# Sorting positions by tile before the first layer, instead of scattering rows to slots after the last

## The chip, the core and the metric

The kernel runs on one core of a Trainium2 chip. The metric is the device time of one execution in microseconds (us). The profile gives for one profiled execution the span from the first to the last instruction on that core, and what each engine and each transfer did in it. PE is TensorE, DVE is VectorE, ACT is ScalarE, POOL is GpSimd, and SP is SyncE, which only issues transfers here.

## The reference

x has 2 batches of 1024 positions of 256 features; the context has 77 rows of 192 features in each batch. Four blocks follow one another, each added to its input:

```python
x = x + xattn0(layernorm(x), ctx)      # 16 heads of 16
x = x + ffn0(layernorm(x))             # one expert, 256 -> 1024 -> 256, then its own layernorm
x = x + xattn1(layernorm(x), ctx)      # one head of 256, layernorms inside
# ffn1: a matrix per position, chosen by the position alone
scores = pe @ sign(tile_sigs).T        # (1024, 8)
idx = argmax(scores, axis=-1)          # one of 8 tiles for each position, the same in both batches
y_all = einsum('bsd,tod->bsto', layernorm(x), W) + b
x = x + y_all[b, s, idx[s]]
```

The last block has 8 matrices of 256 x 256. A position needs only the product with the matrix of its tile. Everything is float32. Which tile a position has depends on `tile_sigs`, an input, so it is worked out on the chip, but it does not depend on x.

## The kernel before, in words

The 2048 positions are worked on in 8 chunks of 256 (`NC`), two blocks of 128 each (`NI`); chunks 0 to 3 are batch 0, chunks 4 to 7 batch 1. Each chunk passes through `attention0`, `ffn0`, `attention1`, and then through `to_slots` (chunks 0 to 6) or `by_every_tile` (chunk 7). These are Python generators with a place in a queue (`begin`); `run` takes the generator with the lowest place, emits its next instructions, and puts it back at the place that it yields. Chunk c has places near 2c, so neighbouring chunks overlap. The instructions' order on each engine is then set by the framework's scheduler from this order of emission; at run time each engine follows its own order strictly, and so do SP's and POOL's transfers.

Names for reading the trace: `ps_q` (L580) is the query product of attention 0, `sc` its scores, `mx`, `pr`, `sm` its softmax, `pT` the transposed weights, `ps_o` and `ps_y` its output; `ps_h` and `ps_eo` (L676, L688) are the two products of ffn0; `xT_b`, `ps_s`, `ps_y1` belong to attention 1. `moments` makes mean and reciprocal deviation `rs` of a layernorm, on POOL (L196, L197) except for the last two chunks, where a chain of small VectorE operations does it (`inverse_root`). A suffix a, f, g, b or h on `rs`, `n` and `xT` says which layernorm it is: before attention 0, before and inside ffn0, before attention 1, before the last block.

x is loaded by plain transfers, chunk by chunk (L83). The first context (keys `kbd`, values `vbd`) is prepared beside chunk 0; the values of batch 1 take a path through HBM (`v_rows` to `ext`) and five multiplications on POOL (L321). The second context (`second_context`) and the choice of tiles (`choices`) come in the time of chunks 1 to 3.

The last block sorts rows by tile. `choices` computes for every position the row of a slot, so that each slot block of 128 rows holds one tile only. `zeros` writes zeros to all slots in HBM. `to_slots` scatters each block's normalized rows, its x plus bias, and its row number to the slots by an indirect transfer from POOL. `block` loads a slot block and the matrix of its tile (SP reads the matrix's row number from SBUF into a register, L777), transposes it on PE (`ps_yT`, L803), copies it on ACT (L805), multiplies (`ps_t`, L809), adds (L814) and scatters 128 rows to the output (L173). There are 15 such blocks for batch 0 and 13 for batch 1. The last chunk isn't sorted: `by_every_tile` multiplies it by all 8 matrices (`ps_z`, L834) and picks by a mask (L840); its weights `every` are one 2 MB load.

## Time and profile before

| what | value |
|---|---|
| times of three runs | 337.59, 339.75, 340.19 us; median 339.75 |
| the profiled execution: time / span | 340.51 us / 338.4 us |
| mean granted TensorE clock | 0.967 of full speed |
| busy: PE, DVE, ACT, POOL | 301.8, 211.0, 141.4, 130.6 us |
| PE products of the last block: ps_t, ps_yT, ps_z busy in the trace | 16.9 + 6.9 + 8.2, 11.6, 15.0 us |
| indirect transfers on POOL: out, slots, bias | 28 x 0.980, 14 x 1.019, 8 x 1.115 us |
| moved by DMA | 39.69 MB, mean 117 GB/s |

A busy time says how long an engine had something in work, not that it was the limit. An idle engine matters only where the chain of work that ends last runs through it. The three busy times of `ps_t` belong to three buffers for its weights (wt, wt_vbd, wt_w); matmuls overlap, so their busy times add up to more than the time that they take in a row. Each float32 product is two instructions in the trace: 128x128 by 128x256 in a full pipeline takes 0.43 us.

### The profile page before, as it was taken

How to read it: one execution, taken by the hardware profiler on the slowest of the kernel's cores; microseconds unless marked ns; L12 is line 12 of the kernel's file. 1: busy time of each engine (PE TensorE's matmuls, PEld its weight loads, DVE VectorE, ACT ScalarE, POOL GpSimd, SP SyncE). 2: the span in 40 equal slices, each digit the busy share in tenths (PEclk: the TensorE clock that was granted, in tenths of full speed). 3: DMA queues.
4: the chain of work that ended last, by engine and by line, in shares of the span. 5: the costliest groups of instructions: out<-in, count | busy, mean ns of one | idle time of the engine just before them, and what ended most of it. 6: DMA issues, size and time to landing. Idle time of an engine off the chain costs nothing.

```text
span 338.4 us, 6080 instructions
## 1 busy us (share of the span) xinstructions
PE 301.8 (89%) x2144; PEld 247.6 (73%) x2144; DVE 211.0 (62%) x624; ACT 141.4 (42%) x309; POOL 130.6 (39%) x183
## 2 busy tenths in 40 slices
PE   2979789999799899999999999999799996578995
PEld 2656568888488678877887888888688885455884
DVE  2278884695459657929757784894346659326343
ACT  2246566535234457365464744645324421212110
POOL 3104560424003458346435512432652716415422
PEclk9999999999899999999999999999999999559999
DMA  7597299999401302701000100250845687164510
GB/s 198 197 334 184 104 241 139 213 158 76 39 0 44 115 13 93 255 32 45 20 2 0 64 0 2 69 182 1 252 133 183 204 253 254 64 186 128 167 34 16
DMA packets 23209, 39.69 MB, mean 117 GB/s; under 512 B 2669, under 2 KB 9354, under 8 KB 23180
## 3 DMA queue, kind: packets, MB, share of 16 engines
q1 hardware_dynamic: 19788, 32.22, 38.3%
q0 software_dynamic: 2848, 6.57, 5.9%
q10 hardware_dynamic: 544, 0.52, 0.5%
q8 instruction: 17, 0.28, 0.4%
q14 instruction: 12, 0.10, 0.1%
HBM read 25.52 MB, written 15.62 MB: 122 GB/s over the span
## 4 chain that ended last, share of the span: by engine, by line
PE 63%; DVE 18%; issue 7%; DMA 4%; POOL 3%; ACT 2%; SPq 1%; POOLq 0%; ACTq 0%
PE ps_eo L688 15%; PE ps_h L676 11%; PE ps_t L809 5%; PE ps_pT L634 4%; PE ps_z L834 4%; PE ps_y L656 4%; DVE mx L608 3%; PE ps_q L580 3%; DVE pr L610 3%; PE ps_o L643 2%; PE ps_s L721 2%; PE sc L599 2%; PE ps_y L746 2%; DMA wt<-in_wrow 2%; DMA wk<-in_wk 2%
## 5 line engine op out<-in xcount | busy, mean ns | idle before, releaser
L676 PE MATMUL ps_h<-xT_f,w 128*128 128x256 f32 x256 | 63.3, 390 | 3.0 <-issue 2.1
L688 PE MATMUL ps_eo<-w,hT 128*128 128x256 f32 x256 | 58.4, 381 | 1.9 <-ACT hT L681 1.9
L676 PEld LDWEIGHTS ps_h<-xT_f,w 128*128 128x128 f32 x256 | 47.0, 192 | 11.6 <-issue 4.5
L688 PEld LDWEIGHTS ps_eo<-w,hT 128*128 128x128 f32 x256 | 47.5, 190 | 8.3 <-ACT hT L681 2.3
L173 POOL DMA_INDIRECT out<-res,blk x28 | 27.4, 980 | 38.1 <-DVE res L814 14.5
L681 ACT ACTIVATE hT<-ps_h,cols 128x256 f32<-128x256 f32 x64 | 27.1, 466 | 30.7 <-PE ps_h L676 30.6
L614 ACT ACTIVATE pr<-pr 128x616 f32<-128x616 f32 x32 | 22.9, 717 | 37.5 <-DVE pr L610 37.5
L608 DVE TENSOR_REDUCE mx<-sc 128x8 f32<-128x616 f32 x32 | 25.2, 788 | 5.3 <-PE sc L599 5.3
L635 ACT COPY pT<-ps_pT 128x512 f32<-128x512 f32 x48 | 25.4, 595 | 6.2 <-PE ps_pT L634 6.2
L750 DVE SCALAR_TENSOR_TENSOR x<-ps_y,sm,x 128x256 f32<-128x256 f32 x16 | 7.1, 479 | 29.7 <-PE ps_y L746 29.7
L617 DVE TENSOR_REDUCE sm<-pr 128x8 f32<-128x616 f32 x32 | 24.6, 781 | 1.4 <-ACT pr L614 1.0
L610 DVE TENSOR_TENSOR pr<-sc,mx 128x616 f32<-128x616 f32 x32 | 25.2, 787 | 0.2
L805 ACT COPY yT<-ps_yT 128x256 f32<-128x256 f32 x28 | 10.4, 371 | 35.2 <-PE ps_yT L803 35.2
L634 PE MATMUL ps_pT<-ident,pr 128*128 128x128 f32 x160 | 21.0, 274 | 3.7 <-ACT pr L614 2.0
L566 POOL TENSOR_TENSOR x<-x,rows 128x512 f32<-128x512 f32 x16 | 21.0, 1321 | 8.3 <-ACT n_a L227 5.4
L634 PEld LDWEIGHTS ps_pT<-ident,pr 128*128 128x128 f32 x160 | 18.1, 141 | 5.9 <-ACT pr L614 2.5
L656 PE MATMUL ps_y<-wo,oT 128*128 128x256 f32 x64 | 17.4, 394 | 4.5 <-DVE oT L650 4.5
L765 POOL TENSOR_TENSOR both<-x,bias 128x256 f32<-128x256 f32 x14 | 9.9, 725 | 24.6 <-DVE x L750 24.5
L643 PE MATMUL ps_o<-pT,vbd 128*32 128x128 f32 x512 | 19.0, 283 | 0.1
L643 PEld LDWEIGHTS ps_o<-pT,vbd 128*32 128x32 f32 x512 | 14.4, 112 | 5.7 <-issue 4.5
L809 PE MATMUL ps_t<-wt,yT 128*128 128x256 f32 x60 | 16.9, 403 | 1.8 <-ACT yT L805 1.3
L173 POOL DMA_INDIRECT slots<-both,to x14 | 14.3, 1019 | 9.2 <-DVE both L232 2.7
(196 smaller groups left out, 545.8 us busy)
## 6 DMA issues: line engine op xcount, KB each, us to landing
blk<-slots SPq DMA_DIRECT2D x28, 256.5 KB
slots<-zero SPq DMA_DIRECT2D x1, 3847.5 KB
wt<-in_wrow SPq DMA_DIRECT2D x15, 256.0 KB
slots<-zero SPq DMA_DIRECT2D x1, 3334.5 KB
w<-in_w SPq DMA_DIRECT2D x2, 1024.0 KB
every<-in_wrow SPq DMA_DIRECT2D x1, 2048.0 KB
wt_w<-in_wrow SPq DMA_DIRECT2D x8, 256.0 KB
x<-in_x SPq DMA_DIRECT2D x7, 256.0 KB
```

The costliest lines, as they stand in the source:

```text
L173: i = nc.gpsimd.indirect_dma_start(out=to, out_offset=bass.IndirectOffsetOnAxis(ap=index, axis=0), in_=rows_in, in_offset=None, bounds_che ...
L608: nc.vector.tensor_reduce(mx, scv, AX.X, ALU.max)
L610: nc.vector.tensor_tensor(p8.rearrange("p (j h l) -> p j h l", j=4, l=L), scv, mx.unsqueeze(3).to_broadcast([P, 4, 2, L]), ALU.subtract,)
L617: nc.vector.tensor_reduce(sm[:, g * 8 : g * 8 + 8], pr[:, g, :G8].rearrange("p (h l) -> p h l", l=L), AX.X, ALU.add,)
L634: nc.tensor.transpose(ps[:, j * P : (j + 1) * P], srcs[4 * n + j], ident)
L635: nc.scalar.copy(pT[:, n].rearrange("p j t -> p (j t)"), ps)
L643: nc.tensor.matmul(ps[32 * m : 32 * m + 32, g * P : (g + 1) * P], vbd[:, e, n, g, 32 * m : 32 * m + 32], pTs[:, g * NK + n, :], start=n == ...
L656: nc.tensor.matmul(ps[:, :D], oT[:, g, :], wo[:, g, :], start=g == 0, stop=g == KC - 1)
L676: nc.tensor.matmul(ps[:, j, :], w1[:, k, (f + j) * P : (f + j + 1) * P], tT[:, k, :], start=k == 0, stop=k == KC - 1,)
L681: nc.scalar.activation(hT[-1][:, j, :], ps[:, j, :], AF.Relu, bias=col(C_B1 + f + j))
L688: nc.tensor.matmul(ps[:, :D], hT[f // 2][:, f % 2, i * P : (i + 1) * P], w2[:, f, :], start=f == 0, stop=f == F // P - 1,)
L809: nc.tensor.matmul(ps[:, :D], yT[:, k * P : (k + 1) * P], w[:, k * D : (k + 1) * D], start=k == 0, stop=k == KC - 1,)
```

## The change

The choice of tiles comes first (place -4), with the second context beside it. From the one-hot choice, `choices` computes the sorted order of the 1024 positions: where each position goes (`at`), and by a product of two comparisons which position stands at each place (`who`). x is then gathered in sorted order by indirect transfers on POOL (`rows_of_x`, two per chunk), in place of the plain loads; chunks alternate between the batches (`e = c % B`). All four layers work on sorted positions.

In sorted order a block of 128 positions has its tiles next to one another, so a batch has at most 8 + 7 = 15 pairs of a block and a tile (`NJ`). `pairs` computes the block (`block_i`), the matrix (`tile_i`) and the output rows (`to`) of each pair; rows that belong to another pair get a number beyond the output and are not written. `to_pairs` normalizes a chunk, transposes it on PE and keeps the result (`nT_of`) and x plus bias (`y_of`) in SBUF for all blocks. `pair` then copies the block's nT and y from there to its own buffers, by transfers whose source is given by a register, loads the matrix, multiplies, adds, and scatters to the output. The slots, their zeros, the blocks' transposes, and the dense products with `every` are gone. The 30 pairs are issued on SP as their chunk is done, and their products stand at the places `LATE`, near the end.

```diff
-    xs = [load("x_0", [P, NI, D], x_in[0], nc.scalar)]
-    xs += [load(f"x_{c}", [P, NI, D], x_in[c]) for c in range(3, NC)]
+    xs = [work.tile([P, NI, D], F32, tag="x", name=f"x_{c}", bufs=6) for c in range(NC)]
...
+    def rows_of_x(c):
+        e, s0 = c % B, c // B * NI
+        for i in range(NI):
+            gather(
+                xs[c][:, i, :], a["x"].rearrange("b s d -> (b s) d"),
+                chosen["who"][:, e, s0 + i : s0 + i + 1],
+            )
...
-    def to_slots(c, x):
+    def to_pairs(c, x):
         b = 2 * c
-        e, s0 = divmod(c * NI, NS)
+        e, s0 = c % B, c // B * NI
         m = moments(x, NI, f"h{c}", vector=c >= NC - 2)
+        written(
+            nc.gpsimd.tensor_tensor(
+                y_of[e][:, s0 : s0 + NI, :], x, bias[:, s0 : s0 + NI, :], ALU.add
+            ), e,
+        )
         yield b + 8.3
...
+        n = normed(x, NI, D, f"h{c}", m, act=True)
         yield b + 8.6
...
+        ps = bank(f"ps_xT_h{c}").rearrange("p (i k t) -> p i k t", i=NI, k=KC)
+        for i in range(NI):
+            for k in range(KC):
+                nc.tensor.transpose(ps[:, i, k, :], n[:, i, k * P : (k + 1) * P], ident)
+        written(
+            nc.scalar.copy(
+                nT_of[e][:, s0 : s0 + NI, :], ps.rearrange("p i k t -> p i (k t)")
+            ), e,
+        )
+
+    def pair(e, p, place):
+        n = f"{e}_{p}"
+        w = work.tile([P, KC * D], F32, tag="wt", name=f"wt_{n}", bufs=WT)
+        nT = work.tile([P, KC * P], F32, tag="nTp", name=f"nTp_{n}", bufs=NP_)
+        y = work.tile([P, D], F32, tag="yp", name=f"yp_{n}", bufs=NP_)
         first = nc.sync.value_load(
-            chosen["row"][0:1, e, j : j + 1], min_val=0, max_val=(NT - 1) * P
+            chosen["row"][0:1, p : p + 1], min_val=0, max_val=(NT - 1) * P
         )
         nc.sync.dma_start(w, a["wrow"][bass.ds(first, P), :])
...
+        lo, hi = max(0, p - NT + 1), min(p, NS - 1)
+        at = nc.sync.value_load(chosen["block"][0:1, p : p + 1], min_val=lo, max_val=hi)
+        readers[e].append(nc.sync.dma_start(y, y_of[e][:, bass.ds(at, 1), :]).ins)
+        readers[e].append(nc.sync.dma_start(nT, nT_of[e][:, bass.ds(at, 1), :]).ins)
+        yield place
         ps = bank(f"ps_t_{n}")
         for k in range(KC):
             nc.tensor.matmul(
-                ps[:, :D], yT[:, k * P : (k + 1) * P], w[:, k * D : (k + 1) * D],
+                ps[:, :D], nT[:, k * P : (k + 1) * P], w[:, k * D : (k + 1) * D],
                 start=k == 0, stop=k == KC - 1,
             )
...
+        r = work.tile([P, D], F32, tag="res", name=f"res_{n}", bufs=4)
+        nc.vector.tensor_tensor(r, ps[:, :D], y, ALU.add)
+        scatter(out, chosen["to"][:, e, p : p + 1], r, "out", B * S - 1)
+
+    LATE = (19.0, 19.2, 19.4, 19.6, 19.8, 20.0, 21.0, 22.8)
 
     for c in range(NC):
         begin(-1.4 if c == 1 else 2 * c - 2, attention0(c, xs[c]))
         begin(2 * c + 2.7, ffn0(c, xs[c]))
         begin(2 * c + 6.1, attention1(c, xs[c]))
-        begin(2 * c + 8.1, (to_slots if c < NC - 1 else by_every_tile)(c, xs[c]))
...
+        begin(2 * c + 8.1, to_pairs(c, xs[c]))
+    begin(-4, paced(-4, 0.4, choices()))
+    begin(-3.9, paced(-3.9, 0.4, first_context()))
+    begin(-3.7, paced(-3.7, 0.4, second_context()))
+    begin(-2.45, once(rows_of_x, 0))
+    begin(-2.4, once(rows_of_x, 1))
+    begin(-3.2, paced(-3.2, 0.2, values()))
+    begin(-1.8, paced(-1.8, 0.1, values_by_head()))
+    for c in range(2, NC):
+        begin((-0.6, 0, 1, 2, 8.7, 10.7)[c - 2], once(rows_of_x, c))
...
+    for c in range(NC):
+        e, j = c % B, c // B
+        ps = range(NI * j, NI * j + NI) if j < NC // B - 1 else range(NI * j, NJ)
+        for n, p in enumerate(ps):
+            begin(2 * c + 8.7 + 0.02 * n, pair(e, p, LATE[c] + 0.1 * n))
```

`WT` is 8 and `NP_` is 5. The computations inside `choices` and `pairs` are small operations on tables of 8 to 128 columns: some 30 on VectorE in `choices`, the comparisons `hot` among them, and some 18 in `pairs`.

## The prediction

> **What bounds the kernel now.** I read the cores view first (one core, span 338.4 us, granted clock 0.967), then the page's busy slices, then the table of windows with its borders at TensorE's milestones: the start of each chunk's query product ps_q, the end of the last attention-0 block (240.84), the end of chunk 7's second FFN product ps_eo (277.44), the end.
>
> ```profile
> core 0: us, PE busy (x) PEld busy (x) DVE busy (x) ACT busy (x) POOL busy (x), PEclk, DMA share, GB/s
> 0.00:29.07 29.07, 19.86 (x127) 14.22 (x127) 12.96 (x37) 10.54 (x18) 5.11 (x23) 1.00 0.84 244
> 45.16:73.85 28.69, 27.92 (x231) 23.53 (x230) 20.71 (x44) 15.07 (x31) 7.65 (x10) 1.00 1.04 185
> 73.85:111.42 37.57, 35.44 (x268) 28.64 (x267) 25.22 (x77) 15.07 (x31) 7.75 (x10) 0.95 0.49 53
> 171.28:199.43 28.15, 27.77 (x229) 23.33 (x228) 19.75 (x54) 15.90 (x35) 11.93 (x17) 1.00 0.05 20
> 199.43:240.84 41.41, 41.03 (x322) 34.47 (x320) 26.73 (x75) 20.21 (x47) 15.78 (x24) 1.00 0.22 64
> 240.84:277.44 36.60, 34.20 (x180) 29.95 (x180) 20.02 (x75) 13.33 (x33) 17.14 (x20) 1.00 0.67 211
> 277.44:338.40 60.96, 46.10 (x205) 36.86 (x203) 30.69 (x115) 9.92 (x26) 23.12 (x24) 0.85 0.40 125
> ```
>
> From 45 to 277 us PE is full: 27.77 of 28.15 us in a steady chunk, so work taken off PE there is time. The ends are chains: until the second ps_q PE computes 19.9 of 29.1 us, much of it cold, and after 277.44 it has 46.1 of 61.0 us at clock 0.85. DMA is full only early. The timeline shows the prices I need:
>
> ```profile
> 10.79 3.78 PE L580 MATMUL ps_q<-xT_a,wq 128*128 128x256 f32 x8 [0.68 <-ACT xT_a L257]
> 29.07 1.99 PE L580 MATMUL ps_q<-xT_a,wq 128*128 128x256 f32 x8
> 37.31 2.96 POOL L321 TENSOR_TENSOR vbd<-ext,cols 128x256 f32<-128x256 f32 x5 [2.48 <-DMA ext<-v_rows]
> 114.14 1.31 POOL L557 DMA_INDIRECT bias<-in_b,tid  x1 [0.18 <-issue]
> 115.75 0.95 POOL L557 DMA_INDIRECT bias<-in_b,tid  x1 [0.30 <-issue]
> 116.73 0.73 POOL L197 TENSOR_TENSOR rs_a<-rs_a,mhalf 128x2 f32<-128x2 f32 x1
> 290.32 0.47 PE L254 MATMUL ps_xT_b<-ident,n_b 128*128 128x128 f32 x1 [4.24 <-ACT n_b L227]
> 292.96 1.99 PE L721 MATMUL ps_s<-wqkg,xT_b 128*128 128x77 f32 x8
> ```
>
> A gather occupies POOL for about a microsecond and the next instruction starts only after it: rs_a stood behind two of them. After a 4.24 us gap PE runs at half pace (ps_s 1.99 us, elsewhere 1.05). The chain that ended last gives landings, and shows that it ended in the dense products ps_z:
>
> ```profile
> 281.00 5.15 DMA wt<-in_wrow
> 304.79 2.15 DMA out<-res,blk
> 310.32 2.83 DMA blk<-slots
> 331.20 3.47 PE ps_z L834 x16
> ```
>
> and the groups of the lines view the mean of one gather of 128 rows:
>
> ```profile
> L557 POOL DMA_INDIRECT bias<-in_b,tid x8 | 8.9, 1115 | 2.7 <-issue 1.5 <-DVE tid L478 1.2
> ```
>
> **What the Trainium skill says.** "TensorE: Matmul & The Clock Gate", section "Part 1: The HAM clock gate", says that PE falls to half clock after an idle window of about 3.4 us and rises again after as long a busy one; the 4.24 us gap and the doubled ps_s agree. Its opening table calls the queues of VectorE, ScalarE and GpSimd strict FIFO; rs_a behind the gathers agrees. "DMA: Bandwidth & Descriptors", section "Anatomy of one DMA", fits a software DMA by 2.0 us plus bytes over 436 GB/s: an estimate of 2.3 us for 128 KB. The nearest row, 2.83 us for a 256 KB block, is of that order.
>
> **The change part by part.** Instruction orders are those of the built kernel.
>
> *Head, until the second ps_q: 29.07 becomes about 57.0, +27.9 us.* x no longer arrives by a plain load (BN_STATS at 4.5); its row numbers must be computed first. Step by step: peT lands near 4 us; 16 choice products at cold pace, twice the 0.12 us each that they take warm, to 7.8; transposes of ctx to 8.5; VectorE copies cxT, does the statistics of ctx, then five choice operations of 0.2 us, to 10.9. PE then has, in its order, the count, ps_k (2.4 us cold, as before) and ps_v (2.7 before) ahead of ps_ahead: 17.2. Sixteen small VectorE operations, eight comparisons of 0.25 us, the who products and two more operations: the row numbers stand at about 22.4. POOL then does, in order, four gathers for x_0 and x_1 (1.115 busy + 0.30 issue = 1.41 each: 28.1), the five vbd products (2.96: 31.1; their ext rows need v_rows written and read back, each near 4.7 us as ext took, so by 27), five gathers for x_2, x_3 and half of x_4 (38.1), the first half of rs_a0, one more gather, and the power 0.72: 40.5. The statistics of x_0 wait since about 31, so the gathers queued ahead, not the data, set this. From the scale to the second ps_q: shift and normalization 1.4, transposes and copy 0.9, the cold ps_q 3.8 (the row at 10.79), qT behind two normalizations on ACT, scores to 8.2, then 8.2 for max, subtraction, exponential, sum, reciprocal, pT and ps_o: 16.5 us, so 57.0. The cover is none: nothing before x can run but the contexts, which are done by then. Ends: if row numbers stand at 18, +23; if POOL loses 2 us to ext, +30.
>
> *Middle, second to eighth ps_q: 170.4 becomes 158.6, -11.8 us.* The second context and the choices leave (PE 2.8 us in the stage from 45.16, 6.7 in that from 73.85, with some 2.5 us of waits on their VectorE rows): 28.7 to 26.3 and 37.6 to 28.6. Per chunk the transposes of n_h come in (0.43 us); ScalarE's 1.7 us for n_h and its copy lie in its idle half, and VectorE loses 0.86 us. POOL exchanges the slot scatters for the gathers of x_5 to x_7. Stages: 15.5, 26.3, 28.6, 30.0, 29.6, 28.6. Ends -9 (the gathers delay more scales) and -14. The 7.2 MB of zeros and `every` leave DMA, worth nothing where PE bounds.
>
> *Eighth ps_q to the end of ps_eo of chunk 7: 78.0 becomes 70.2, -7.8.* Nine blocks leave (9 x (0.865 product + 0.22 transpose) = 9.8), two pairs (1.7) and three transpositions (1.3) come in: -6.8; the 1.9 us that ps_eo waited for hT behind the slot scatters falls to 0.9. Ends -5 and -9: without blocks to fill it, PE now waits on the chain of g6 and b6, by my schedule under 1 us.
>
> *From there to the end: 61.0 becomes 57.0, -4.0.* Off PE go the rest of the blocks and 32 dense products (13.8 us); 28 pairs of 0.865 us stay. But these pairs are fed late: nTp and yp have five buffers, wt eight, and SP, in order, stops at the sixth nTp until the first pair's product is done, so 22 pairs load here, three transfers each at 0.5 us of SP (five wt_vbd issues took 2.78). Counted from the end of ps_eo: VectorE's statistics of b7 wait for res of pair 1_4, to 10; the two root chains, the normalizations and copies to 18; ps_s1_7 cold 2; the nine pairs of batch 0 stand in PE ahead of ps_y1_7, the first half cold, the last waiting for its copy: 30.3; y1 and the h7 chain, cold again, to 38.6; then nine copies (2.83 us to the first) and nine pairs. There the scatters bind: 9 x 1.28 us on POOL, 2.15 to land, about 0.8 to close: 57.0. The copies inside SBUF are in no row: from 2.3 us (the skill's estimate) to 5.15 (a wt load in a crowd); four round trips lie in series, so -0.6 to +10.9. I take 2.83.
>
> **Sum.** +27.9 - 11.8 - 7.8 - 4.0 = +4.3 us on the profiled execution's 340.51 us: 344.8; on the median 339.75 it is 344.05. I take 344.5.
>
> **The rivals.**
> *The copies land ahead of need (faster).* If a copy takes little over 1.5 us, no in-order engine waits for one in the last stage and PE keeps its clock: ps_s1_7 -1.0, batch 0's pairs -2.4, the h7 chain -0.5, the first copy -0.5, the last pairs -0.9, VectorE's wait before b7 -3.0: -8.3, so 336.2. For it: out landed in 2.15 with its POOL time inside. Against: 2.83 and 5.15. It decides below 1.5 us.
> *The head is cheaper (no change).* If PE warms during the choice products and the VectorE operations overlap, row numbers stand at 18 and the sum is near zero: 339.7. For it: the products are close together; against: PE was cold until 15.7 us before.
> *The copies are slow.* At 5.15 us: 355.4. For it: 22 pairs x 0.52 MB plus 3.9 MB of scatters, 15 MB in 60 us, is the 253 GB/s of the busiest slices; against: the waits are spread.
>
> **How the numbers follow.** Forecast 0.40, slow copies 0.12, cheaper head 0.20, early copies 0.28. Slower by over 1% (about what a measurement of this kernel can tell from no change) 0.52, within 0.20, faster 0.28. The forecast's own range is 341 to 350. Low copies with a somewhat cheaper head reach 334; the slow copies 356.
>
> **What would show it.** Right: the second ps_q starts near 57, POOL full of DMA_INDIRECT from 22 to 40 with rs_a behind them, steady chunks of 28.6, and after chunk 7's ps_eo PE at clock near 0.8, pairs waiting for nTp. Wrong: rs_a before 35, a last stage under 50 us or over 66, or PE waiting in the middle for gathers.

## The result: 361.3 us, 6.7% slower

The changed kernel takes 361.32 us (median; 360.79 to 362.27) against 339.68 us before: a ratio of 1.0668, interval 1.0612 to 1.0724. The forecast was 344.5 us with a range of 334 to 356, so the direction was right, with a stated chance of 0.52, and the size was not: the loss is 21.6 us, over four times the 4.8 us that were forecast. The profiled execution took 361.73 us, its span is 359.6 us (338.4 before), its granted clock 0.927 (0.967 before). The one profiled execution of the kernel before, 340.51 us, was a slow one, above all its other runs (337.59 to 340.19 us), and the profiled executions shown below lie up to 3.8 us from the medians of their runs, so small differences between stages of two profiles carry little.

The windows view of the changed kernel, cut at the same milestones as before: the second ps_q at 64.09, the next ones, the eighth at 223.73, the end of chunk 7's second FFN product ps_eo at 294.35, the end. Two stages of the middle, 137.04 to 166.63 and 195.18 to 223.73, are left out here. After the stretch come its length, then busy time and instruction count by engine.

```profile
core 0: us, PE busy (x) PEld busy (x) DVE busy (x) ACT busy (x) POOL busy (x), PEclk, DMA share, GB/s
0.00:64.09 64.09, 44.55 (x213) 34.62 (x213) 29.45 (x101) 11.86 (x22) 21.92 (x42) 0.84 0.51 157
64.09:79.57 15.48, 13.01 (x148) 10.25 (x145) 11.11 (x27) 8.63 (x18) 5.05 (x8) 0.98 0.01 2
79.57:105.13 25.56, 25.35 (x211) 21.17 (x210) 17.25 (x36) 14.10 (x29) 7.74 (x8) 1.00 0.03 7
105.13:137.04 31.91, 28.48 (x223) 23.47 (x221) 19.14 (x50) 15.81 (x33) 12.83 (x16) 0.95 0.11 22
166.63:195.18 28.55, 28.35 (x233) 23.79 (x231) 19.12 (x57) 16.88 (x36) 11.57 (x16) 1.00 0.10 29
223.73:294.35 70.62, 68.72 (x465) 58.62 (x464) 42.30 (x140) 33.88 (x73) 19.47 (x27) 1.00 0.05 15
294.35:359.60 65.25, 37.62 (x144) 28.86 (x143) 27.29 (x106) 5.88 (x12) 30.06 (x30) 0.78 0.63 207
```

Set against the four terms of the prediction:

| term | before | after | change | forecast |
|---|---|---|---|---|
| start to second ps_q | 29.07 | 64.09 | +35.0 | +27.9 |
| second to eighth ps_q | 170.36 | 159.64 | -10.7 | -11.8 |
| eighth ps_q to end of ps_eo of chunk 7 | 78.01 | 70.62 | -7.4 | -7.8 |
| from there to the end | 60.96 | 65.25 | +4.3 | -4.0 |
| span | 338.4 | 359.6 | +21.2 | +4.3 |

The two stretches in which PE is full came out as worked. Both ends, which are chains of waits, were sized too short: 7.1 us in the head and 8.3 us in the tail.

The timeline of the head (start, duration, engine, line, output<-input, and in brackets the idle time before the work and what ended it):

```profile
24.48 1.29 PE L509 MATMUL ps_who<-his,hot 128*128 128x8 f32 x6
25.81 0.24 DVE L515 TENSOR_SCALAR who<-ps_who 128x8 int32<-128x8 f32 x2 [1.24 <-PE ps_who L509]
26.28 1.21 POOL L585 DMA_INDIRECT x<-in_x,who  x1 [15.92 <-DVE who L515]
27.79 0.95 POOL L585 DMA_INDIRECT x<-in_x,who  x1 [0.30 <-issue]
40.85 1.01 POOL L585 DMA_INDIRECT x<-in_x,who  x1 [0.16 <-issue]
41.89 0.74 POOL L193 TENSOR_TENSOR rs_a<-rs_a,mhalf 128x2 f32<-128x2 f32 x1
42.66 0.16 DVE L218 SCALAR_TENSOR_TENSOR sh_a<-mv_a,rs_a 128x2 f32<-128x2 f32 x1 [5.08 <-POOL rs_a L193]
46.30 3.78 PE L616 MATMUL ps_q<-xT_a,wq 128*128 128x256 f32 x8 [0.68 <-ACT xT_a L253]
60.20 2.08 PE L364 MATMUL ps_bv<-wo,bvb 128*128 128x256 f32 x4
64.09 1.19 PE L616 MATMUL ps_q<-xT_a,wq 128*128 128x256 f32 x3
```

The shape is the one forecast: the row numbers stand (25.8), POOL starts its gathers at once, and x_0's inverse root rs_a comes only behind ten of them. VectorE waited 5.08 us for that root.

The timeline of the tail:

```profile
313.63 1.99 PE L757 MATMUL ps_s<-wqkg,xT_b 128*128 128x77 f32 x8 [0.68 <-ACT xT_b L253]
316.96 6.39 PE L839 MATMUL ps_t<-wt,nTp 128*128 128x256 f32 x20 [1.33 <-DVE pr L768]
327.18 1.10 PE L839 MATMUL ps_t<-wt,nTp 128*128 128x256 f32 x4 [1.03 <-DMA nTp<-nT]
335.81 1.18 PE L816 MATMUL ps_xT_h<-ident,n_h 128*128 128x128 f32 x4 [6.66 <-ACT n_h L223]
339.73 9.53 PE L839 MATMUL ps_t<-wt,nTp 128*128 128x256 f32 x32 [2.74 <-DMA nTp<-nT]
342.52 0.99 POOL L169 DMA_INDIRECT out<-res,to  x1 [9.86 <-DVE res L844]
350.89 0.42 DVE L844 TENSOR_TENSOR res<-ps_t,yp 128x256 f32<-128x256 f32 x1 [1.59 <-DMA out<-res,to]
353.35 0.97 POOL L169 DMA_INDIRECT out<-res,to  x1 [0.30 <-issue]
```

Three things stand in series here: the nine pairs of chunk 6 (316.96 to 328.3), then chunk 7's own chain through y1 and h7 with PE idle for 6.66 us at a stretch, then the nine pairs of chunk 7, whose ninth scatter starts at 353.35.

### The profile page after: what moved, and what is told of

The parts are those of the page before. It is cut to its first block, busy times and chain, and to the rows that moved or that the text cites. A ratio compares the mean times of both kernels' runs of the same rounds, so it can differ in the third digit from the quotient of the medians.

```text
span 359.6 us, 6049 instructions
## 1 busy us (share of the span) xinstructions
PE 303.1 (84%) x2080; PEld 248.3 (69%) x2080; DVE 203.4 (57%) x617; ACT 140.9 (39%) x292; POOL 132.3 (37%) x177
## 4 chain that ended last, share of the span: by engine, by line
PE 55%; issue 15%; DVE 13%; POOL 8%; DMA 4%; ACT 3%; POOLq 1%; SPq 0%; DVEq 0%; ACTq 0%
PE ps_eo L724 14%; PE ps_h L712 11%; PE ps_pT L670 4%; PE ps_q L616 4%; PE ps_y L692 4%; PE ps_o L679 3%; PE sc L635 3%; POOL out L169 3%; DVE mx L644 3%; POOL x L585 2%; PE ps_s L757 2%; DMA out<-res,to 2%; DVE pr L646 2%; PE ps_y L782 1%; PE ps_xT_a L250 1%
## 5 line engine op out<-in xcount | busy, mean ns | idle before, releaser
L169 POOL DMA_INDIRECT out<-res,to x30 | 29.6, 985 | 38.6 <-DVE res L844 30.3
L839 PE MATMUL ps_t<-wt,nTp 128*128 128x256 f32 x120 | 32.5, 426 | 9.5 <-DMA nTp<-nT 5.5
L644 DVE TENSOR_REDUCE mx<-sc 128x8 f32<-128x616 f32 x32 | 25.2, 787 | 20.9 <-PE sc L635 20.9
L839 PEld LDWEIGHTS ps_t<-wt,nTp 128*128 128x128 f32 x120 | 24.9, 216 | 15.5 <-issue 6.9
L844 DVE TENSOR_TENSOR res<-ps_t,yp 128x256 f32<-128x256 f32 x30 | 12.7, 424 | 24.5 <-PE ps_t L839 17.9
L670 PE MATMUL ps_pT<-ident,pr 128*128 128x128 f32 x160 | 21.8, 282 | 3.6 <-ACT pr L650 2.5
L585 POOL DMA_INDIRECT x<-in_x,who x16 | 16.0, 998 | 19.8 <-DVE who L515 15.9
L806 POOL TENSOR_TENSOR y<-x,bias 128x512 f32<-128x512 f32 x8 | 10.2, 1275 | 34.8 <-DVE x L786 34.8
L192 POOL TENSOR_SCALAR rs_f<-mv_f 128x2 f32<-128x2 f32 x8 | 1.7, 218 | 51.4 <-DVE mv_f L185 51.4
```

Source lines behind the costliest of these rows:

```text
L169: i = nc.gpsimd.indirect_dma_start(out=to, out_offset=bass.IndirectOffsetOnAxis(ap=index, axis=0), in_=rows_in, in_offset=None, bounds_che ...
L585: nc.gpsimd.indirect_dma_start(out=to, out_offset=None, in_=src, in_offset=bass.IndirectOffsetOnAxis(ap=index, axis=0),)
L644: nc.vector.tensor_reduce(mx, scv, AX.X, ALU.max)
L670: nc.tensor.transpose(ps[:, j * P : (j + 1) * P], srcs[4 * n + j], ident)
L839: nc.tensor.matmul(ps[:, :D], nT[:, k * P : (k + 1) * P], w[:, k * D : (k + 1) * D], start=k == 0, stop=k == KC - 1,)
```

## The experiments

All are edits of the changed kernel. Each ratio is against runs of the kernel before on the same chip. The last stage of one and the same code took 65.25 us in the profile above and 69.8 us in another set of runs (`control`). So tails are compared only inside one set; where one is set beside a profile above, it is said. Heads are compared by start times, which repeat: the second ps_q came at 64.09 and at 63.55.

### Which half of the change costs: x by plain loads (h_plain)

```diff
+    def load_x(c, eng=nc.sync):
+        e, s0 = c % B, c // B * NI
+        i = eng.dma_start(xs[c], rows_of(a["x"][e, s0 * P : s0 * P + CH]))
...
+    load_x(0, nc.scalar)
...
-    begin(-4, paced(-4, 0.4, choices()))
-    begin(-3.9, paced(-3.9, 0.4, first_context()))
-    begin(-3.7, paced(-3.7, 0.4, second_context()))
-    begin(-2.45, once(rows_of_x, 0))
...
+    begin(2.5, paced(2.5, 0.4, choices()))
+    begin(-1.95, paced(-1.95, 0.4, first_context()))
+    begin(4.2, paced(4.2, 0.35, second_context()))
...
```

This kernel leaves the sorting out: chunks hold the positions in their own order while the pairs are still those of the sorted order, so its output is not the reference's. It serves as a measure of time alone; the number and size of products and transfers of the pairs stay the same.

> The pairs stay; the sorting of x is left out: every chunk takes its positions in their own order by plain loads, x_0 first, and the contexts, the choice and the values go back to the places that they had in the kernel before. Theory A (the loss is the start, which x's row numbers hold up, and the middle only gives back what was moved into the start): second ps_q at 29 to 31 us, second to eighth ps_q near 170 us as before, the last two stages as in the changed kernel (70.5 and 65.4), so 336 to 339 us in all, 22 to 25 below the changed kernel. Rival B (the pairs themselves cost time in the middle, through POOL and SP): second to eighth ps_q over 178, 345 or more.

345.3 us, ratio 1.0174 (1.0083 to 1.0264). Its windows:

```profile
0.00:29.22 29.22, 20.20 (x126) 14.46 (x126) 12.96 (x37) 10.54 (x18) 5.01 (x22) 1.00 0.82 246
48.11:85.50 37.39, 35.01 (x252) 30.47 (x251) 25.08 (x78) 14.69 (x30) 7.81 (x10) 0.86 0.13 33
202.87:273.50 70.63, 68.72 (x465) 58.62 (x464) 42.25 (x140) 33.85 (x73) 19.50 (x27) 1.00 0.05 15
273.50:340.60 67.10, 38.87 (x144) 29.39 (x143) 26.25 (x106) 5.88 (x12) 30.14 (x30) 0.75 0.62 201
```

The head is back at 29.22, and the second context and the choices are back in the middle (the stage of 37.39 us): second to eighth ps_q is 173.65 against 159.64. So the sorted start costs 34.9 us at the head and gives 14.0 back in the middle, 20.9 us net in the profiles; the medians of the two sets differ by 16 us (361.3 and 345.3). Pairs in place of slots and dense products, taken alone, aren't a gain either: against the kernel before, +3.3 us in the middle, -7.4 where blocks leave and +6.1 in the tail make +2.2 with the head's 0.15 (the tails are of two sets, so the +6.1 is the least certain of these). The prediction had expected this part to be a gain at both of its places. The run met neither expectation: the head and the stage before the tail came as theory A has them, the middle 3.7 us and the last stage 1.7 us longer.

### Is the head a matter of queue order? (h_pool, h_stat, h_rows, h_fix)

POOL's part of the head is 16.8 us between the row numbers and rs_a_0, and most of it serves later chunks. `h_pool` fills the head's POOL queue in program order instead of by the planner's times:

```diff
-    run(0, {mybir.EngineType.DVE})
+    run(0, {mybir.EngineType.DVE, mybir.EngineType.Pool})
```

> One edit: until place 0 POOL too runs in program order, so that the scale rs_a of chunk 0 stands ahead of the vbd products and the gathers of x_2 to x_4. Theory A (POOL's queue holds chunk 0 up, but VectorE's statistics, at 36.5 us behind the second context, come next): rs_a done near 38.3 instead of 42.6, the second ps_q 4 us earlier, 357 us. Rival B (the gathers moved behind are needed soon, and later chunks give the time back): 360 to 362. Rival C (the queue was the only hold): 9 us earlier, 352.

First ps_q 38.66 (46.30 before the edit), second 58.73, third 77.53; 366.01 us, ratio 1.0762 (1.0651 to 1.0872). The first product gained 7.6 us, as the queue says it must. The second kept 5.4 of it, and the stage that follows, 15.48 us in the changed kernel, took 18.80, so the third product gained only 2.0. The total lies above all that was expected for it. But the changed kernel itself was not run in this set, and the last stage took 70.6 us here, so the totals of these runs don't say what the head gained. The end of ps_eo says more: 294.35 and 292.52 in two profiles of the changed kernel, 293.15 in `h_pool`, 290.53 in `h_stat`, 289.28 in `h_rows` and 291.80 in `h_fix`.

`h_stat` adds that block 0's statistics are placed ahead:

```diff
-        begin(-1.4 if c == 1 else 2 * c - 2, attention0(c, xs[c]))
+        begin((-2.3, -1.4)[c] if c < 2 else 2 * c - 2, attention0(c, xs[c]))
```

> As the run with POOL in program order, and chunk 0's statistics start at place -2.3 instead of -2.0, ahead of the second context's products with wqT and wo1 on VectorE. Theory A: statistics at 31.5 us when x_0 has landed, rs_a done near 33.5, first ps_q at 37 instead of 46.3, second ps_q at 55, 352 us. Rival B (given back in later chunks): 357 or more.

38.70 and 60.52; 362.42 us, ratio 1.0643 (1.0533 to 1.0753). What holds the second ps_q now is in the timeline of VectorE:

```profile
49.39 0.43 DVE L183 BATCH_NORM_STATS2 st_a<-x 128x6 f32<-128x256 f32 x1 [5.99 <-DMA x<-in_x,who]
49.73 0.78 DVE L646 TENSOR_TENSOR pr<-sc,mx 128x616 f32<-128x616 f32 x1
```

The statistics of a later chunk stand in VectorE's queue ahead of the softmax of chunk 0, and their gather landed late: 5.99 us in which VectorE stood before work whose data were there (the scores and their maximum were done by 43.4).

`h_rows` adds that the choices run ahead of the contexts (the second context from -3.15, the values from -2.95):

```diff
-    begin(-4, paced(-4, 0.4, choices()))
+    begin(-4, paced(-4, 0.2, choices()))
-    begin(-3.9, paced(-3.9, 0.4, first_context()))
+    begin(-3.9, paced(-3.9, 0.9, first_context()))
...
-    begin(-2.45, once(rows_of_x, 0))
+    begin(-3.3, once(rows_of_x, 0))
...
```

> As the last, and the choice goes ahead of both contexts and the values on PE and VectorE (choices in steps of 0.2 places, first context's second step at -3.0, values from -2.95, second context from -3.15 in steps of 0.83, gathers of x_0 and x_1 at -3.3). Theory A (the row numbers are late because ps_k and ps_v stand ahead of ps_ahead): row numbers at 17 to 19 us instead of 25.8, first ps_q at 31 to 34, second at 49 to 53, 347 to 350 us. Rival B (the contexts' cold products, some 15 us, only move into the chain of chunk 0): second ps_q no earlier than 55, 352 or more.

Row numbers at 20.5 instead of 25.8, first ps_q 34.58, second 59.98; 359.61 us, ratio 1.057 (1.0478 to 1.0663). Again the first moved (by 4.1) and the second hardly (0.5).

`h_fix` moves what stood in VectorE's way in those two: the gathers of x_2 early, the statistics ahead of vbd, the row of biases ahead of chunk 0 (and the second context in steps of 1.1 places instead of 0.83).

```diff
-        begin((-0.6, 0, 1, 2, 8.7, 10.7)[c - 2], once(rows_of_x, c))
+        begin((-2.8, 0, 1, 2, 8.7, 10.7)[c - 2], once(rows_of_x, c))
-    begin(1.1, once(row_of_biases))
+    begin(-1.9, once(row_of_biases))
...
-        begin((-2.3, -1.4)[c] if c < 2 else 2 * c - 2, attention0(c, xs[c]))
+        begin((-2.9, -1.4)[c] if c < 2 else 2 * c - 2, attention0(c, xs[c]))
```

> The start again, with what the last trace of it showed taken away: there x_2's gathers landed at 49 us, and VectorE, whose statistics of x_2 stood ahead of block 0's softmax, waited for them. Now x_2's gathers come right behind rs_a of chunk 0 and ahead of vbd, chunk 0's statistics ahead of the vbd products on VectorE, the row of biases ahead of chunk 0, and the second context in steps of 1.1 places. The tail is that of the changed kernel, so it serves as its measure on this chip. Theory A (queue order in the start, no resource, holds chunk 0): first ps_q at 31 to 33 us, second at 47 to 51 (64 in the changed kernel), end of chunk 7's ps_eo at 277 to 281 (294), 13 to 16 us less in all. Rival B (the contexts' cold products only move behind chunk 0's start): second ps_q at 56 or later, 5 to 8 us less.

35.57 and 60.81; 357.39 us, ratio 1.0575 (1.053 to 1.0619). The gain hoped for didn't come; each hold was replaced by another of the same kind:

```profile
32.09 0.42 DVE L365 TENSOR_TENSOR rows<-ps_bv,rows 128x256 f32<-128x256 f32 x1 [0.90 <-PE ps_bv L364]
32.43 0.15 DVE L218 SCALAR_TENSOR_TENSOR sh_a<-mv_a,rs_a 128x2 f32<-128x2 f32 x1
47.22 0.16 DVE L218 SCALAR_TENSOR_TENSOR sh_a<-mv_a,rs_a 128x2 f32<-128x2 f32 x1 [6.38 <-POOL rs_a L193]
48.29 0.79 DVE L646 TENSOR_TENSOR pr<-sc,mx 128x616 f32<-128x616 f32 x1
```

rs_a_0 was ready at 28.1, but its shift stood in VectorE's queue behind the row of biases (32.09), and at 47.22 the shift of a later chunk waited 6.38 us for an inverse root that stood on POOL behind four gathers, again ahead of chunk 0's softmax. So moving POOL alone helped little here: VectorE, in order, had a POOL-fed instruction of a later chunk in front.

### The head with PE's queue in order too (h_vec)

PE too gets program order (so that the products for the row numbers come ahead of ps_k and ps_v), and x_2's inverse root is computed on VectorE instead of POOL. The values and the row of biases come behind chunk 0's start, values_by_head at 0.95 and the second context in steps of 1.3 places.

```diff
-    run(0, {mybir.EngineType.DVE})
+    run(0, {mybir.EngineType.DVE, mybir.EngineType.Pool, mybir.EngineType.PE})
-        m = moments(x, NI, f"a{c}")
+        m = moments(x, NI, f"a{c}", vector=c == 2)
...
-    begin(-2.95, paced(-2.95, 0.1, values()))
+    begin(0.02, paced(0.02, 0.1, values()))
-    begin(-1.9, once(row_of_biases))
+    begin(0.55, once(row_of_biases))
```

> The start a third time; the tail is the changed kernel's. In the last run of it VectorE stood 6.4 us at the shift of x_2, whose power was behind four gathers on POOL, and 4 us at the row of biases ahead of chunk 0's shift. Now until place 0 PE too runs in program order (all ps_who ahead of ps_k), x_2's inverse root is computed on VectorE, the values and the row of biases come beside block 0's softmax, and the second context in steps of 1.3 places. Theory A (in-order waits of VectorE and PE for gathers, not any engine's load, held the start): row numbers at 17 us, first ps_q at 28 to 31, second at 46 to 51, end of chunk 7's ps_eo at 279 to 284, ratio 1.015 to 1.03. Rival B (the work that moved behind chunk 0 has to be done before chunk 1 anyway): second ps_q at 56 or later, ratio over 1.04.

```profile
17.80 0.24 DVE L515 TENSOR_SCALAR who<-ps_who 128x8 int32<-128x8 f32 x2 [1.99 <-PE ps_who L509]
25.34 0.16 DVE L218 SCALAR_TENSOR_TENSOR sh_a<-mv_a,rs_a 128x2 f32<-128x2 f32 x1 [0.34 <-POOL rs_a L193]
30.73 3.78 PE L616 MATMUL ps_q<-xT_a,wq 128*128 128x256 f32 x8 [3.15 <-ACT xT_a L253]
```

Row numbers at 17.8, ps_q at 30.73 and 48.68, the end of ps_eo at 282.17 instead of 294.35: the head is down by 15.4 us, and 12.2 of it are still there after the middle. That is the gain that the four runs ahead had missed. It comes from the edits together; which of them it needs was not tested one by one. 353.5 us, ratio 1.0392 (1.0316 to 1.0469), above what was expected for it: its unchanged last stage took 71.4 us in this set. With 48.68 the head still costs 19.6 us more than before. In this trace 17.8 us go by until the row numbers are known and 7.5 us more until the shift that uses x_0's scale; in the kernel before that shift stood at 6.92.

### The tail: copies, result places, order (t_direct, t_res, t_late6res)

These ran beside `control`, the changed kernel itself: 365.99 us, ratio 1.0801 (1.0718 to 1.0885), last stage 69.8 us.

> The changed kernel itself, on the chip of these runs: 360 to 363 us if the chips agree. With the POOL order of the first series the last stage (end of ps_eo of chunk 7 to the end) took 70 us instead of 65.3; if that is the chip, it shows here too (366 us); if not, it is something that those edits did.

`t_direct` leaves out the choice of a pair's block: each pair reads a fixed block in place, without the two copies inside SBUF, so its output is not the reference's. SP also has two transfers and one register to load less for each pair:

```diff
-        nT = work.tile([P, KC * P], F32, tag="nTp", name=f"nTp_{n}", bufs=NP_)
-        y = work.tile([P, D], F32, tag="yp", name=f"yp_{n}", bufs=NP_)
+        nT = nT_of[e][:, min(p, NS - 1), :]
+        y = y_of[e][:, min(p, NS - 1), :]
...
-        lo, hi = max(0, p - NT + 1), min(p, NS - 1)
-        at = nc.sync.value_load(chosen["block"][0:1, p : p + 1], min_val=lo, max_val=hi)
-        readers[e].append(nc.sync.dma_start(y, y_of[e][:, bass.ds(at, 1), :]).ins)
-        readers[e].append(nc.sync.dma_start(nT, nT_of[e][:, bass.ds(at, 1), :]).ins)
```

> The choice of a pair's block is left out: each pair multiplies nT and adds y of a fixed block where they lie, so that no copy nTp or yp is made and 60 transfers of 128 KB go; the rows of weights are still chosen and loaded. Theory C (round trips of the copies set the last stage, as the prediction had it): 8 us less, 352 to 354. Theory S (the scatters set it: one per pair at 1.28 us on POOL, four result buffers, each held until its scatter has landed, and VectorE in order behind them): only the waits for nTp in the trace go (1.0 + 2.7 + 1.8 us), 355 to 358.

359.23 us, ratio 1.0583 (1.0506 to 1.0659), 6.8 us less than `control`, which lies between what the two theories expected and doesn't decide between them; last stage 65.0. The groups of the lines view for the tail, `control` first, `t_direct` second, with the idle time ahead of the pairs' products:

```profile
L839 PE MATMUL ps_t<-wt,nTp 128*128 128x256 f32 x112 | 33.1, 453 | 11.2 <-DMA nTp<-nT 5.5 <-DVE res L844 2.9 <-issue 2.8
L835 PE MATMUL ps_t<-wt,nT 128*128 128x256 f32 x116 | 31.1, 427 | 1.8 <-issue 1.1 <-ACT nT L818 0.7
```

The idle time of PE ahead of the pairs fell by 9.4 us (11.2 less 1.8), of which 5.5 are put down to nTp; the last stage fell by 4.8. About half of that stands ahead of chunk 7's transposes of h7, which start 43.1 us after ps_eo here and 45.3 us after it in `control`, and half behind them.

`t_res` gives the pairs of chunks 4 to 6 result places of their own (chunks 4 and 5 in the space of ext, chunk 6 in that of vbd; `result` gives the place) in place of the four shared ones:

```diff
-        r = work.tile([P, D], F32, tag="res", name=f"res_{n}", bufs=4)
+        r = result(c, i)
```

> One edit: the results of the 13 pairs of chunks 4, 5 and 6 get a place of their own each (in the space of ext and vbd, which is free by then) instead of the four rotating buffers res. Theory S: VectorE no longer waits there for a scatter to land; the statistics of b7 and the update of x by y1_7 come 1 to 3 us sooner each, 356 to 359 us, and less spread between runs. Theory C: no change, 361.

365.43 us, ratio 1.0768 (1.0669 to 1.0866), last stage 70.8: no gain. The 6.6 us that VectorE waits for scattered results in the changed kernel lie beside other waits.

`t_late6res` is `t_res` with the nine pairs of chunk 6 moved behind ps_y1 of chunk 7:

```diff
-    LATE = (19.0, 19.2, 19.4, 19.6, 19.8, 20.0, 21.0, 22.8)
+    LATE = (19.0, 19.2, 19.4, 19.6, 19.8, 20.0, 21.85, 22.8)
```

> The last edit, and the nine pairs of chunk 6 (batch 0) move on PE from ahead of ps_y1_7 to behind it (place 21.0 becomes 21.85), beside chunk 7's last normalization. Theory S with order (the nine pairs and their scatters stood in series ahead of chunk 7's chain): ps_y1_7 9 us sooner, the copies of nT_7 some 7 us sooner, 351 to 354 us. Rival D (POOL's scatters then stand ahead of the addition y of chunk 7 and of the last nine scatters, so they take the time back): 357 or more.

368.29 us, ratio 1.0861 (1.0782 to 1.0939): 2.3 us more than `control`, though ps_y1_7 came at 320.5 instead of 330.1. What it won there it lost behind. The waits of SP's queue in the tail:

```profile
SPq L848 <- PE ps_t L852: 7.8, 3, 5.1
```

SP stood 5.1 us at one transfer whose buffer came free only when the delayed pairs had been computed; then it still had 13 copies of nTp to issue. Three transfers per pair take SP some 0.68 us each, as the changed kernel's own timeline of SP shows:

```profile
300.00 0.49 SPq L834 DMA_DIRECT2D yp<-y  x1
300.69 0.48 SPq L835 DMA_DIRECT2D nTp<-nT  x1
301.36 0.45 SPq L831 DMA_DIRECT2D wt<-in_wrow  x1
```

That is 2.0 us per pair, where a scatter takes 1.28. In `t_late6res` the copies nTp start at 338.93, 340.94, 342.94 and 344.94, and the last nine pairs take 18.4 us on PE (339.87 to 358.30). With this feed the order gained nothing.

### One copy per pair, alone and with the order (t_merge, t_mergelate)

```diff
-    nT_of = [const.tile([P, NS, KC * P], F32, tag=f"nT_{e}", name=f"nT_{e}") for e in range(B)]
-    y_of = [const.tile([P, NS, D], F32, tag=f"y_{e}", name=f"y_{e}") for e in range(B)]
+    ny_of = [const.tile([P, NS, KC * P + D], F32, tag=f"ny_{e}", name=f"ny_{e}") for e in range(B)]
...
-        readers[e].append(nc.sync.dma_start(y, y_of[e][:, bass.ds(at, 1), :]).ins)
-        readers[e].append(nc.sync.dma_start(nT, nT_of[e][:, bass.ds(at, 1), :]).ins)
+        readers[e].append(nc.sync.dma_start(ny, ny_of[e][:, bass.ds(at, 1), :]).ins)
```

> nT and y of a block lie side by side in one tile, and a pair fetches both in one copy of 256 KB: two transfers per pair on SP instead of three, the same bytes. Theory Q (SP's queue sets the tail: each transfer takes 0.68 us there with its registers, so three make 2.0 us per pair against 0.87 on PE and 1.28 on POOL): 1.36 us per pair, 3 to 6 us less than the changed kernel. Theory C (the time from issue to landing): the single copy is twice as large, so 0 to 2 us more. The start is unchanged.

361.75 us, ratio 1.0712 (1.0665 to 1.0759), last stage 67.0 against 65.9 of `h_fix`, whose tail is unchanged, in the same set: fewer transfers alone gain nothing, against the 3 to 6 us that theory Q expected. `t_mergelate` joins it with the edits of `t_late6res`:

> The single copy, results of chunks 4 to 6 in places of their own, and the nine pairs of chunk 6 behind ps_y1_7 on PE. Without the single copy the last two edits lost 2 us, as SP stood 5 us at a full buffer and then had 14 pairs to load at 2.0 us each. Theory Q: with 1.36 us per pair the move of the nine pairs pays, 8 to 12 us less than the changed kernel. If POOL's scatters or landings bind instead: 0 to 4 us less.

355.84 us, ratio 1.0531 (1.0485 to 1.0577), last stage 60.45: 5.9 us less than `t_merge`. The same order that lost 2.3 us when SP fed three transfers per pair wins with two: its copies start 1.2 to 1.5 us apart there (336.32, 337.80, 339.11, 340.34) where they started 2.0 us apart. Neither edit is worth anything by itself, which is why single edits in the tail read as "not the cause". What the result places add to the two was not tested alone.

### Together (all1, all2, all3, all5)

`all1` is the head of `h_fix` with the tail of `t_mergelate`, `all2` the head of `h_vec` with that tail.

> The start of the first of these four runs with the tail of the third. If the two are independent, as the full middle between them suggests, the gains add: 21 to 28 us less than the changed kernel, at or just below the kernel before (ratio 0.99 to 1.01). If the tail eats gains of the start (DMA and SP arrive earlier but not freer): ratio 1.02 to 1.04.

351.49 us, ratio 1.0413 (1.0361 to 1.0465), span 348.6. Its gain on `t_mergelate` in the profiles, 5.3 us, is the earlier end of ps_eo (288.74 against 293.45) and 0.6 of tail: the ends add up. It stays behind the 21 to 28 us that were expected, since neither end had gained what was hoped for it.

> This start with the tail of the single copies and the nine pairs of chunk 6 behind ps_y1_7. With theory A and independent ends: 7 us under the sum before (end of ps_eo at 280, tail 60): 340 to 344 us, ratio 1.00 to 1.02. Rival B: ratio 1.035 to 1.045 as in the last run of both ends.

346.35 us, ratio 1.023 (1.016 to 1.03), end of ps_eo at 278.64, last stage 63.9 (60.45 for the same tail in `t_mergelate`'s set).

`all3` spreads the pairs of chunks 2 to 5 too, into the idle times of chunk 7's chain:

```diff
-    LATE = (19.0, 19.2, 19.4, 19.6, 19.8, 20.0, 21.85, 22.8)
+    LATE = (19.0, 19.2, 20.15, 20.4, 20.65, 21.1, 21.85, 22.8)
```

> As the last, and the pairs of chunks 2 to 5 move as well: behind the statistics of b7, its normalization, its transposes and its scores (places 20.15, 20.4, 20.65, 21.1). Theory S with order (pairs ahead of chunk 7's chain stand in series with it, at POOL's 1.28 us each): the statistics of b7 2 to 4 us sooner, 3 us less than the run above. If SP's queue feeds them no sooner: the same within 1 us.

341.02 us, ratio 1.0049 (1.0017 to 1.008), last stage 57.8.

`all5` also loads the weights of eight of the last nine pairs early, into the space of w1 and w2, which are free by then; spreads the bias gathers; and puts ACT into program order in the head, with ps_v ahead of chunk 0.

```diff
...
+            if c == NC - 1 and n < 8:
+                begin(20.3 + 0.02 * n, once(rows_ahead, c, n, p))
...
-        begin(5 + 0.4 * s, once(lambda s=s: gather(bias[:, s, :], a["b"], chosen["tid"][:, s : s + 1])))
+        begin(6 + 3.6 * (s // 2) + 0.8 * (s % 2), once(lambda s=s: gather(bias[:, s, :], a["b"], chosen["tid"][:, s : s + 1])))
```

> The last version with what its trace still showed as waits. ScalarE too runs in program order until place 0 (there the copy of xT_0 stood 2.5 us behind the normalization of x_1), and ps_v comes into the idle time of PE ahead of chunk 0; the eight gathers of the bias are spread, two per chunk pair, instead of standing together ahead of POOL's scales (the stage from the fourth to the fifth ps_q took 32.6 us with them, 28.5 to 29.6 is a stage without); the weights of eight of the last nine pairs are loaded early into the space of w1 and w2 (SP stood 6 us at weight buffers ahead of the last copies). Theory A+S (queue order at both ends): second ps_q at 45 to 47, fourth to fifth ps_q 30, last stage 54 to 57, 331 to 336 us, ratio 0.975 to 0.99. Rival (the ends are at their floor, each wait removed uncovers another): ratio 1.00 to 1.005 as before.

335.57 us against 337.44 before, ratio 0.9917 (0.9889 to 0.9945): just under the kernel before, by 0.8%, and some 7% under the changed one. It stays short of the 0.975 to 0.99 that were expected. Its windows, from an execution that took 339.32 us:

```profile
0.00:49.24 49.24, 35.86 (x187) 28.46 (x187) 25.62 (x104) 10.89 (x20) 21.33 (x40) 0.83 0.59 186
49.24:209.50 160.26, 156.46 (x1292) 129.03 (x1289) 109.60 (x281) 90.45 (x187) 57.56 (x75) 0.99 0.08 22
209.50:280.16 70.66, 68.75 (x465) 58.61 (x464) 42.29 (x140) 33.90 (x73) 22.90 (x30) 1.00 0.08 23
280.16:337.20 57.04, 35.47 (x144) 27.40 (x143) 25.58 (x106) 5.88 (x12) 29.88 (x30) 0.88 0.66 233
```

Against the profile of the kernel before: +20.2 in the head, -10.1, -7.4, and -3.9 in the tail. The head is no shorter than in `all3` (second ps_q at 49.24 and 48.29), so ACT's order gained nothing there. The tail of 57.0 us that was forecast for the change is there, but it took five edits to get it: one copy per pair, result places, two changes of order, and weights loaded early.

## Why the prediction was wrong in size

Two stages of its sum failed. The head was put at 57.0 us and took 64.09, above all because the 16.5 us from the scale to the second ps_q were 21.4. The stage from ps_eo to the end was put at 57.0 us, a gain of 4.0, and took 65.25, a loss of 4.3; in other sets this stage, unedited, took up to 71.4. The order of events was right in both.

**Head, +35.0 where +27.9 was forecast.** The mechanism was right to the instruction: row numbers, then POOL's queue, then one inverse root behind gathers of other chunks, nothing to cover it (x_0's statistics were done at 37.5 and not at 31, still ahead of POOL). Three terms of its sum were off. *"The row numbers stand at about 22.4"*: they stood at 25.8, +3.4. The products that count, ps_ahead, ended at 18.1 instead of 17.2, behind ps_v (3.62 us with its waits, 2.7 assumed), and the who products that follow didn't run as one burst: PE took them in five pieces from 20.12 to 25.77 with ps_v and transposes of the context between; `h_rows` and `h_vec` show the same products done at 20.5 and 17.8 once they come first. *POOL to 40.5*: 18.1 us were forecast from row numbers to rs_a_0 and 16.8 were needed, since a gather took 0.95 us and 0.30 to the next, 1.25 and not 1.41; so the start of the chain was late by only 2.1. *"From the scale to the second ps_q ... 16.5 us"*: it took 21.4 (42.66 to 64.09), +4.9, and this is the largest error. It was summed from single pieces: the scores were done after 9.1 us (8.2 in the sum), and what follows them took 12.4 us (8.2). The pieces left out the second head group's softmax on VectorE, the row of biases on PE (2.08 us at 60.20) and the waits between engines. The trace of before had the whole stretch in one piece, from the shift that uses x_0's scale to the second ps_q at 29.07:

```profile
6.92 0.16 DVE L222 SCALAR_TENSOR_TENSOR sh_a<-mv_a,rs_a 128x2 f32<-128x2 f32 x1 [0.67 <-POOL rs_a L197]
```

That is 22.15 us. A difference of two start times was to hand, and would have been right within 0.7 us, though the two stretches don't hold quite the same work (ps_v stands in it before). The half pace of PE in the head, which the prediction calls cold, is read from durations (the first ps_q 3.78 us for eight products, later ones 1.99), not from the PEclk column, which shows 1.00 there.

**Middle, -10.7 (forecast -11.8), and the eighth ps_q to ps_eo, -7.4 (-7.8).** Both right. Where PE was full, instructions times duration gave the time: the steady stage of 28.55 us was forecast as 28.6, the one from 64.09 as 15.5 (15.48), the next as 26.3 (25.56). One stage missed, 31.91 for 28.6; that the sum is off by only 1.1 us is in part luck, since three other stages came out 0.4 to 1.1 us shorter. The traces show what the sum lacked, a wait of PE for hT and the pace of the eight products behind it. Here are the changed kernel, `control` and `h_fix`, whose stages took 31.91, 30.34 and 32.90 us:

```profile
114.57 2.55 PE L712 MATMUL ps_h<-xT_f,w 128*128 128x256 f32 x8 [2.58 <-ACT hT L717]
114.29 1.99 PE L712 MATMUL ps_h<-xT_f,w 128*128 128x256 f32 x8 [2.59 <-ACT hT L717]
111.05 3.78 PE L712 MATMUL ps_h<-xT_f,w 128*128 128x256 f32 x8 [2.58 <-ACT hT L717]
```

The wait is the same in all runs with the sorted start (2.4 to 2.6 us), and the stage is longer where the products behind it run at half pace: 29.9 to 30.3 us at 1.99, 32.6 to 32.9 at 3.78. Spreading the bias gathers (`all5`) left a wait of 2.42 us; its stage took 30.73 us with those products at 3.61, some 2 us less than the others at such a pace. Why the pace behind one and the same wait differs is not shown.

**Tail, +4.3 where -4.0 was forecast.** The three bursts and the chain between them are as described, and each was too short. From the end of ps_eo: the nine pairs of batch 0 ended at 33.9 instead of 30.3 (+3.6); from there to the blocks of h7 it took 9.3 instead of 8.3 (+1.0); from there to the end 22.0 instead of 18.4 (+3.6). In the first, ps_s of chunk 7 began at 19.3 and not at 18, the softmax steps between it and the pairs (1.3 us to pr) were not in the sum, and the pairs ran at 1.26 us each with waits for copies. In the last, "then nine copies and nine pairs, there the scatters bind": the first scatter came 4.9 us after the blocks stood (4.0 in the sum), the nine went out at 1.35 us each (342.52 to 353.35) instead of 1.28, and 6.25 us passed from the start of the last to the end, for which 4.2 stood in the sum. The tile view of out gives the landings:

```profile
DMA to landing us min/median/max: 2.1/2.9/5.4
```

2.15 us, the one row that was taken from the chain before, is near the fastest of these and not their middle. The range that the prediction gave for the copies doesn't follow from the 2.83 us that it took: four round trips at 2.3 and at 5.15 us make -2.1 and +9.3, not -0.6 and +10.9.

**The rivals.** *Slow copies*, the one that a result of 361 us points to, isn't what happened: the same view for nTp, from 290 us on, gives

```profile
DMA to landing us min/median/max: 2.0/2.7/3.5
```

so the middle copy took just under the assumed 2.83 us. The estimate of 2.3 us for 128 KB from the fit in the Trainium skill ("DMA: Bandwidth & Descriptors", "Anatomy of one DMA") lies inside this spread, though that fit is given for software DMAs issued from GpSimd, and these copies are issued by SP. The copies matter, 6.8 us by `t_direct`, but not by a slow landing: SP issues three transfers per pair at 0.68 us each, where 0.5 us was assumed. *Early copies* needed 1.5 us, which no copy reached. *Cheaper head* needed row numbers at 18, for a head of +23; in the change as it is they stood at 25.8. `h_vec` has them at 17.8, with the queues changed too, and a head of +19.6; but `h_rows` has them at 20.5 and a head of +30.9. So the rival's condition isn't met, and early row numbers alone don't give its price.

**The signs that the prediction named.** The second ps_q near 57: 64. POOL full of gathers from 22 to 40 with rs_a behind: 26 to 42. Steady chunks of 28.6: 28.55. Clock near 0.8 in the tail: 0.78. A last stage between 50 and 66: 65.25. The signs in the order of events were all there, those in the head on the late side; the change of the last stage came out with the other sign. None of the signs of being wrong showed in this profile, although the size was wrong: the bounds of 50 and 66 us were too wide to tell 57 from 65.25. In `control` the last stage, 69.8 us, lies over them.

## What to carry to other kernels

Where an engine is full, count instructions; where a stretch is a chain, take its length from two start times in the trace that is there, because a sum of pieces leaves out the waits; here it erred short at both ends. Before moving a queue, list what each in-order engine has in front of the first consumer: the head fell by 15.4 us when POOL, VectorE and PE were put in order and later work was moved out of VectorE's way in one run, after four smaller edits had moved the first product by up to 11.7 us and the second by 5.4 at most. The same holds for a tail: a better order needs a feed that keeps up with it, and edits that gain nothing one by one (`t_res`, `t_merge`, `t_late6res`) gave 5.9 us together.

## What the runs showed of the hardware

A gather of 128 rows holds POOL for 0.95 us and a scatter for 0.97, with 0.30 us to the next: 1.25 and 1.28 us in a row (a first gather took up to 1.29). SP needs about 0.68 us for a transfer with an offset from a register; three per pair, 2.0 us, were the pace of the last pairs in `t_late6res`, and two per pair with the same bytes came 1.2 to 1.5 us apart in `t_mergelate`. VectorE stood 5.99 and 6.38 us (`h_stat`, `h_fix`) at an instruction of a later chunk while the current chunk's work was ready behind it. After PE had stood 6.66 us, four transposes took 1.18 us (335.81), where four of that size took 0.66 us in the full middle (104.63); with a granted clock of 0.78 in the last stage this agrees with the gate that the Trainium skill describes, half clock after an idle window of some 3.4 us ("TensorE: Matmul & The Clock Gate", "Part 1: The HAM clock gate"). And the last stage, unchanged, took from 65.25 to 71.4 us between sets of runs, with 69.9 to 71.4 us in the runs on one chip, 69.8 on a second and 65.9 on a third, while the stretch ahead of it, in which PE is full, agreed within 0.1 us in all of them; why isn't settled by these runs.
